# Perceiver of four layers on one core: the first tile's rows, queries, later constants and weights are put in another order where three cross-attentions open

## Chip, cores and metric

The kernel runs on one core of one Trainium2 chip, in fp32. The metric is the device time of one execution in microseconds (us). Engines are named as in the profile: PE (TensorE, matmuls), DVE (VectorE), ACT (ScalarE), POOL (GpSimd), SP (SyncE, which here only issues DMAs). L12 is line 12 of the kernel before; where a line of the changed kernel is meant, the text says so.

## What is computed

The input is x with 16 batches of 64 rows of 256 (1024 tokens) and a context of 16 batches of 1024 rows of 192. Four layers follow each other, each of three parts that add to x:

```python
x = x + L1_xattn(layernorm(x), ctx, ...)   # 16 heads over 1024 keys of the batch
x = x + L1_attn(layernorm(x), ...)
x = x + L1_ffn(layernorm(x), ...)          # 8 experts, top 1
x = x + L2_xattn(layernorm(x), ctx, ...)   # 8 heads of 64
x = x + L2_attn(layernorm(x), ...)         # complex linear recurrence over 64 rows
x = x + L2_ffn(layernorm(x), ...)          # 8 experts, top 2, capacity 160
x = x + L3_xattn(layernorm(x), ctx, ...)   # 8 heads of 64
x = x + L3_attn(layernorm(x), ...)         # convolution, state space with 16 states
x = x + L3_ffn(layernorm(x), ...)          # three dense layers of +1/-1 weights
```

Layer 0 is built alike; its ffn takes the top 2 of 8 experts and adds a shared expert. So each of the three later cross-attentions comes straight after a feed-forward part with experts.

## The kernel before

The tokens lie in SBUF as `xs`, 8 tiles of 128 (two batches each). A feed-forward part with experts writes its results, sorted by expert, to HBM (`ys`). The next stage brings them back: `carry(i)` (L1388) gathers tile i's rows by an indirect DMA that POOL issues (L1386), one per expert choice, two after layer 0 and layer 2 and one after layer 1, and DVE adds each, weighted by its gate, to `xs` (L1395). Then `norm_tile` makes the layernorm's numbers (DVE L154, L156, L158; POOL L160, a power), DVE writes the normalized tile `o`, POOL adds the attention's bias to `xs`, PE transposes `o` (L179), and an evict on DVE or ACT in turn (L62, L64) brings it to SBUF as `hT`.

`L1_xattn` (the opening at L1014) makes, for batch 0, four pieces: `keys(0)`, `values(0)`, `keys(1)`, `values(1)` (matmuls L926, L928 and L940, L947; evicts to `kT` and `v`), with the three turns of `queries(0)` (carry, norm and `o`; transposes and `hT`; matmuls, `qs` and the two DMAs of `qs` L907 that turn it to other partitions) after the second, third and fourth piece. In this opening the order of PE and DVE instructions is the written one, in the loop that follows that of PE only; all other orders are chosen by a scheduler that runs over the program with its own costs, so it may hoist the later tiles' gathers and adds. The loop has 64 steps (16 batches of 4 groups of heads): scores (`sc`, L69), `nmx` on DVE (L223), `p` on ACT (L225), transposes (L235) and their copies `pT` (DVE L239, ACT L237), averages. Batch b+1's four pieces are spread over the steps of batch b, one a step, but step 0 also takes one before its scores. `queries(1)` and `queries(2)` are also given their turns in these steps. The gathered rows rest in four buffers (`back`).

`heads64` (L431) is the cross-attention of layers 2 and 3. For a tile, `normalized(i)` does carry, norm and transposes (the o of all tiles is one buffer), `queries(i)` the matmuls to `qT` (DVE L470), `with_keys(i, n)` turns them by the key weights to `qp` (twice, evicts L62 and L64), then scores with the context itself (L505). In layer 2 (`L2_xattn_attn`, L1728) the stage of the recurrence is made first (`recurrence`, L1739: powers on POOL L1749 and L1752, a chain of small DVE steps L1751 to L1769 and L1781 to L1792 that wraps angles, sine and cosine on ACT) and its steps are then woven in by calls from within heads64. In layer 3 (`state_space`) a block of matmuls, `first()` (32 of them, evicts ACT L1986), goes first; `weights()` issues six DMAs on SP: `L3a_in` 1 MB, `L3a_bc` 64 KB, `L3a_out` 512 KB (L1990) and `k0` 512 KB, `k1` 1 MB, `k2` 256 KB (L1910). Nothing makes these wait but the rooms they write to.

Of the kernel before, what the change touches and what calls it, by code (L numbers as in the profile page):

```python
# [11 lines left out]
F32 = mybir.dt.float32  # L12
# [30 lines left out]
class Net:  # L43
# [387 lines left out]
    def heads64(  # L431
# [5 lines left out]
        nc = self.nc  # L437
        wq, wkT, wv0, wv1, wo, bo, (sels, rb, vT), self.spent = self.pack()
        large = large or self.misc
        qpT, hT = {}, {}  # L440

        nc.gpsimd.iota(
            sels.rearrange("p h (r d) -> p h r d", r=2), pattern=[[1, 4], [32, 2], [0, 64]], base=0,
# [6 lines left out]
        def normalized(i):  # L450

            if i < 2:
                self.carry(i, self.lp.tile([128, 4, D], F32, tag="p", bufs=2, name="p"))
            else:
                self.carry(i, tag="o", bufs=1)
            mv, rs = self.norm_tile(self.xs[:, i, :], 1e-5)
            o = self.lp.tile([128, D], F32, tag="o", bufs=1, name="o")
            nc.vector.tensor_scalar(o, self.xs[:, i, :], mv[:, 0:1], rs, ALU.subtract, ALU.mult)
            nc.gpsimd.tensor_tensor(self.xs[:, i, :], self.xs[:, i, :], bo, ALU.add)
            hT[i] = self.lp.tile([128, 2, 128], F32, tag="hT", bufs=2, name="hT")  # L460
            self.evict(hT[i], self.transposed(o))
# [391 lines left out]
    def L1_xattn(self):  # L853
# [26 lines left out]
            self.mm(ps, [(bv[:, c, :], wo[:, c, :]) for c in range(2)] + [(self.ones[:1, :], bo)])  # L880
            nc.scalar.copy(bias, ps)

        qs = {}

        def queries(i):

            self.carry(i)
            mv, rs = self.norm_tile(self.xs[:, i, :], 1e-5)
            o = self.lp.tile([128, D], F32, tag="o", bufs=2, name="o")
            nc.vector.tensor_scalar(o, self.xs[:, i, :], mv[:, 0:1], rs, ALU.subtract, ALU.mult)  # L890
            nc.gpsimd.tensor_tensor(self.xs[:, i, :], self.xs[:, i, :], bias, ALU.add)
            yield
            hT = self.lp.tile([128, 2, 128], F32, tag="hT", bufs=2, name="hT")
            self.evict(hT, self.transposed(o))
            yield
            ps = self.misc([128, 2, 128])
            for m in range(2):
                self.mm(ps[:, m, :], [(wq[:, c, m * 128 : (m + 1) * 128], hT[:, c, :]) for c in range(2)])
            qs[i] = [self.lp.tile([128, 2, 2, 2, S], F32, tag=f"qs{n}", bufs=3, name=f"qs{n}") for n in range(2)]
            for m in range(2):  # L900
                for h in range(2):
                    nc.vector.tensor_scalar(
                        qs[i][0][:, m, :, h, :], ps[:, m, :].rearrange("p (b s) -> p b s", s=S),
                        self.col("L1x_bq", m), self.pair4[:, h : h + 1], ALU.add, ALU.mult,
                    )
            for r in range(2):
                nc.sync.dma_start(qs[i][1][64 * r : 64 * r + 64], qs[i][0][64 - 64 * r : 128 - 64 * r])  # L907
            yield
# [102 lines left out]

        self.room_t = self.misc

        with self.tc.manual_schedule(engines={mybir.EngineType.PE, mybir.EngineType.DVE}):  # L1014
            biases()
            for piece, turn in zip(keys_values(0), (None, *[queries(0)] * 3)):
                piece()
                if turn is not None:
                    next(turn)
        with self.tc.manual_schedule(engines={mybir.EngineType.PE}):  # L1020
            held, work = None, {}
# [3 lines left out]
            for k in range(len(steps) + 4):  # L1025
# [5 lines left out]
                if k < len(steps):  # L1031
                    b, g = steps[k]
                    if not g:
                        sums = self.lp.tile([128, 8], F32, tag="sums", bufs=3, name="sums")
                        more = keys_values(b + 1) if b + 1 < B else None
                    if not k:
                        more.pop(0)()
                    now = (b, g, scores(b, g, sums), sums)
                for piece in work.pop((k, "early"), ()):
                    piece()  # L1040
# [344 lines left out]
    def gather_rows(self, out, src, at):  # L1385
        return self.nc.gpsimd.indirect_dma_start(out, None, src, bass.IndirectOffsetOnAxis(ap=at, axis=0))  # L1386

    def carry(self, i, room=None, tag="back", bufs=4):  # L1388

        if self.routed is None:  # L1390
            return
        for n, (at, g) in enumerate(zip(self.routed.at, self.routed.gates)):
            y = self.lp.tile([128, D], F32, tag=tag, bufs=bufs, name="back") if room is None else room[:, n, :]
            self.gather_rows(y, self.ys, at[:, i : i + 1])
            self.nc.vector.scalar_tensor_tensor(  # L1395
                self.xs[:, i, :], y, g[:, i : i + 1], self.xs[:, i, :], ALU.mult, ALU.add
            )
# [331 lines left out]
    def L2_xattn_attn(self):  # L1729


        with self.tc.manual_schedule(engines={mybir.EngineType.PE}):
            lru = self.recurrence()
            self.heads64(breathe=lru.go, finished=lru.more)
            self.start_pack(self.at)
            while lru.go():
                pass

    def recurrence(self):  # L1739
        nc = self.nc  # L1740
        s = SimpleNamespace(ready=0, next=0, work=None)
        w = []
# [2 lines left out]
        at = VEC_AT["L2a_logs"]  # L1745
        logs = self.vecs[:, at : at + 3]
        e1 = self.lp.tile([128, 3], F32, name="e1")
        nc.vector.memset(e1, float(np.e))
        nc.gpsimd.tensor_tensor(ex[:, :3], e1, logs, ALU.pow)  # L1749
        neg = self.lp.tile([128, 1], F32, name="neg")  # L1750
# [199 lines left out]
    def state_space(self):  # L1950
# [35 lines left out]
                nc.scalar.copy(w[1][:, :, cols], ps)  # L1986

        def weights():
            for n, to in zip(("in", "bc", "out"), (w[0], w[2], w[3])):
                nc.sync.dma_start(to, self.a[f"L3a_{n}"])  # L1990
            yield
            self.ffn = self.fetch_L3_ffn((self.spent[0], w[4], self.spent[1]))
            yield

        def prepare(k):
# [508 lines left out]
```

## Time and profile before

| what | us |
|---|---|
| three runs | 2837.02, 2842.88, 2844.15 |
| median | 2842.88 |
| the profiled execution | 2838.53 |
| its span, first to last instruction | 2836.7 |
| PE's busy time in it | 2603.1 |
| opening of L1's cross-attention, first keys to the second nmx | 438.4 to 476.3 |
| opening of L2's, last write of expert rows to the first scores | 1221.0 to 1243.9 |
| opening of L3's, the same | 1931.6 to 1959.7 |

The granted clock of TensorE over the span was 0.963 of full. A row of a timeline gives start, duration, engine, line, operation, output and inputs, the number of instructions in it, and in brackets the idle time of the engine before it with what ended it. A row of the DMA view gives the count, the size of each and the median time from issue to landing. An entry of the chain gives the start, the duration and what the end of the kernel hung on in that time.

### The profile page before, as it was taken

The numbers are of one execution on the slowest core, as the hardware profiler recorded it, in microseconds if no ns is written. First come the engines' busy times: TensorE is split into PE (matmuls) and PEld (weight loads), VectorE is DVE, ScalarE is ACT, GpSimd is POOL, SyncE is SP. The second block draws the span as 40 slices with busy tenths as digits, with TensorE's granted clock in tenths as the row PEclk, the third lists the DMA queues.
The fourth block names the chain that finished last, engine by engine and source line by source line (L and its number), as shares of the span: only waits on it lengthen the run. The fifth ranks groups of instructions, "written<-read, shape, count | busy, mean of one in ns | idle before, by whom it ended". The sixth has DMA issues, their size and how long they took to land.

```text
span 2836.7 us, 44734 instructions
## 1 busy us (share of the span) xinstructions
PE 2603.1 (92%) x18116; PEld 1889.9 (67%) x18116; DVE 1399.4 (49%) x2825; ACT 1003.4 (35%) x2114; POOL 311.8 (11%) x429
## 2 busy tenths in 40 slices
PE   7888998999999898979999999698999998998999
PEld 3556895666666686856666666695666665666777
DVE  3556225666666643233434342423344756658692
ACT  1323223555555441222222222122234545455330
POOL 1111333000000112310001000201001000000000
PEclk9988999999999997989999999799999999999999
DMA  8512872100100114801111111463112213121110
GB/s 244 174 49 77 339 271 65 31 27 28 38 27 23 42 38 176 305 25 47 59 58 55 45 49 59 181 239 108 51 49 91 86 49 97 56 76 30 61 45 8
DMA packets 79228, 253.71 MB, mean 89 GB/s; under 512 B 15151, under 2 KB 26954, under 8 KB 69290
## 3 DMA queue, kind: packets, MB, share of 16 engines
q1 hardware_dynamic: 59562, 165.01, 18.0%
q0 software_dynamic: 13312, 80.28, 7.9%
q10 hardware_dynamic: 6144, 5.51, 0.6%
q8 instruction: 145, 2.38, 0.3%
q14 instruction: 65, 0.53, 0.1%
HBM read 233.80 MB, written 14.82 MB: 88 GB/s over the span
## 4 chain that ended last, share of the span: by engine, by line
PE 38%; DVE 9%; ACT 3%; issue 2%; DMA 2%; POOL 1%; SPq 1%; DVEq 0%; ACTq 0%; POOLq 0%
PE sc L505 9%; PE ps_h L69 5%; PE misc L541 4%; PE halves L69 3%; PE misc L69 3%; PE ps_t L519 3%; PE halves L541 3%; PE misc L536 2%; PE gu L69 2%; DVE x L2104 2%; PE halves L2128 2%; PE halves L536 1%; DVE nmx L223 1%; DVE x L2100 1%; DMA rep<-dus 1%
## 5 line engine op out<-in xcount | busy, mean ns | idle before, releaser
L223 DVE TENSOR_REDUCE nmx<-sc 128x1 f32<-128x1024 f32 x264 | 311.7, 1218 | 228.4 <-PE sc L505 144.8
L225 ACT ACTIVATE p<-sc,nmx 128x1024 f32<-128x1024 f32 x264 | 294.2, 1115 | 313.5 <-DVE nmx L223 313.3
L505 PE MATMUL sc<-ctxT,qp 128*128 128x512 f32 (+1 forms) x1024 | 357.5, 603 | 0.0
L505 PEld LDWEIGHTS sc<-ctxT,qp 128*128 128x128 f32 (+1 forms) x1024 | 139.4, 190 | 155.4 <-issue 152.3
L519 PE MATMUL ps_t<-ident,p 128*128 128x128 f32 x1024 | 140.2, 279 | 40.2 <-ACT pT L522 17.3
L2094 ACT ACTIVATE da<-rep,al 128x252 f32<-128x252 f32 x256 | 115.9, 500 | 134.4 <-DVE x L2104 124.2
L519 PEld LDWEIGHTS ps_t<-ident,p 128*128 128x128 f32 x1024 | 115.3, 142 | 65.2 <-ACT pT L522 21.0
L2104 DVE TENSOR_TENSOR_SCAN x<-da,x 128x512 f32<-128x512 f32 x128 | 152.7, 1218 | 2.7 <-ACT da L2094 1.9
L235 PE MATMUL misc<-ident,p 128*128 128x128 f32 x1024 | 137.1, 279 | 7.2 <-ACT p L225 6.8
L522 ACT COPY pT<-ps_t 128x512 f32<-128x512 f32 x166 | 94.0, 587 | 122.0 <-PE ps_t L519 116.1
L235 PEld LDWEIGHTS misc<-ident,p 128*128 128x128 f32 x1024 | 110.1, 141 | 32.7 <-ACT p L225 15.4
L160 POOL TENSOR_TENSOR ln_rs<-ln_ve,nhalf 128x1 f32<-128x1 f32 x80 | 44.9, 567 | 692.8 <-DVE ln_ve L158 611.0
L541 PE MATMUL halves<-pT,ctx 128*128 128x256 f32 x512 | 119.3, 386 | 0.0
L541 PE MATMUL misc<-pT,ctx 128*128 128x256 f32 x512 | 119.1, 386 | 0.0
L237 ACT COPY pT<-misc 128x512 f32<-128x512 f32 x128 | 75.0, 586 | 108.6 <-PE misc L235 108.1
L69 PE MATMUL ps_h<-r,w 128*128 128x256 f32 x512 | 113.4, 381 | 0.0
L2100 DVE TENSOR_TENSOR x<-rep,bc_rep 128x512 f32<-128x512 f32 x128 | 84.7, 687 | 57.9 <-PE halves L2128 55.2
L239 DVE COPY pT<-misc 128x512 f32<-128x512 f32 x128 | 88.3, 690 | 39.7 <-PE misc L235 28.6
L69 PEld LDWEIGHTS ps_h<-r,w 128*128 128x128 f32 x512 | 96.6, 190 | 15.9 <-issue 2.5
L541 PEld LDWEIGHTS halves<-pT,ctx 128*128 128x128 f32 x512 | 94.8, 190 | 17.3 <-issue 5.6
L541 PEld LDWEIGHTS misc<-pT,ctx 128*128 128x128 f32 x512 | 94.6, 190 | 17.1 <-issue 5.5
L69 PE MATMUL po<-wb,hid 128*128 128x256 f32 x440 | 100.3, 379 | 0.0
(500 smaller groups left out, 4504.3 us busy)
## 6 DMA issues: line engine op xcount, KB each, us to landing
ctx<-in_ctx SPq DMA_DIRECT2D x48, 768.0 KB, 4.4
ctxT<-in_ctxT SPq DMA_DIRECT2D x48, 512.0 KB, 3.3
w<-in_L2f_W SPq DMA_DIRECT2D x24, 1024.0 KB, 8.3
rep<-dus SPq DMA_DIRECT2D x256, 64.0 KB, 1.9
ctxT<-in_ctxT SPq DMA_DIRECT2D x16, 768.0 KB, 15.5
ctxT<-in_ctxT SPq DMA_DIRECT2D x96, 128.0 KB, 3.5
ys<-yb ACTq DMA_DIRECT2D x40, 128.0 KB, 5.7
bc_rep<-bcs SPq DMA_DIRECT2D x32, 128.0 KB, 3.0
```

Of the source, the lines that this page charges most:

```text
L69: self.nc.tensor.matmul(out, lhsT, rhs, start=n == 0, stop=n == len(pairs) - 1)
L223: self.nc.vector.tensor_reduce(nmx, sc, AX.X, ALU.max, negate=True)
L225: self.nc.scalar.activation(p, sc, AF.Exp, bias=nmx, accum_out=sums)
L235: self.nc.tensor.transpose(ps[:, u, :], p[:, at : at + 128], self.ident)
L239: self.nc.vector.tensor_copy(pT[:, 0:4, :], ps)
L505: nc.tensor.matmul(sc[u][:, bass.ts(kh, 512)], qp[n][par][rows, h : h + 2, :].rearrange("p h q -> p (h q)"), ctx[0][rows, at], start=n == ...
L519: nc.tensor.transpose(ps[:, t, :], p[:, at : at + 128], self.ident)
L522: nc.scalar.copy(to, ps)
L541: nc.tensor.matmul(o, ck[:, t, :128], pT[:, t].rearrange("p u q -> p (u q)"), start=t == 0, stop=t == NK - 1)
L2094: nc.scalar.activation(da[:, g, :, 1:], now[j][:, 0, :].rearrange("p (b s) -> p b s", s=S)[:, :, 1:], AF.Exp, scale=al[:, col : col + 1],)
L2100: nc.vector.tensor_tensor(h, now[j][:, 1:2, :].to_broadcast([128, 2, CHUNK]), bc[:, 0, states, :], ALU.mult)
L2104: nc.vector.tensor_tensor_scan(flat, da.rearrange("p g b s -> p (g b s)"), flat, 0.0, ALU.mult, ALU.add)
```

## The change

Five edits. `carry` gets an argument `behind`: if it is given, DVE first copies one column of that tile into the room of the gathered rows, so that the gather cannot be issued before that tile exists. heads64 gives tile 1's carry the `o` of tile 0; L1_xattn gives tiles 1 and 2 the `o` of the tile before. In L1_xattn's opening POOL too keeps the written order, and the first turn of `queries(0)` stands ahead of `keys(0)`, the second after `values(0)`, the third after `keys(1)`. In its loop, step 0 no longer takes a piece of batch 1 before its scores, so that steps 0 to 3 take one each. In layer 2 the recurrence is made at the first call from within heads64, and its constant `e1` is first written with a piece of tile 1's `xs`. In layer 3 DVE copies a column of tile 0's `xs` into each of the six rooms before the weights' DMAs. In all DVE has 14 more instructions (4 + 1 + 2 for `behind`, 1 for `e1`, 6 for the rooms), each of one column of 128 or of 128x3; matmuls, transfers and other instructions are the same.

```diff
--- before.py
+++ after.py
@@ -437,7 +437,7 @@
         nc = self.nc
         wq, wkT, wv0, wv1, wo, bo, (sels, rb, vT), self.spent = self.pack()
         large = large or self.misc
-        qpT, hT = {}, {}
+        qpT, hT, os = {}, {}, []
 
         nc.gpsimd.iota(
             sels.rearrange("p h (r d) -> p h r d", r=2), pattern=[[1, 4], [32, 2], [0, 64]], base=0,
@@ -450,11 +450,12 @@
         def normalized(i):
 
             if i < 2:
-                self.carry(i, self.lp.tile([128, 4, D], F32, tag="p", bufs=2, name="p"))
+                self.carry(i, self.lp.tile([128, 4, D], F32, tag="p", bufs=2, name="p"), behind=os[-1] if os else None)
             else:
                 self.carry(i, tag="o", bufs=1)
             mv, rs = self.norm_tile(self.xs[:, i, :], 1e-5)
             o = self.lp.tile([128, D], F32, tag="o", bufs=1, name="o")
+            os.append(o)
             nc.vector.tensor_scalar(o, self.xs[:, i, :], mv[:, 0:1], rs, ALU.subtract, ALU.mult)
             nc.gpsimd.tensor_tensor(self.xs[:, i, :], self.xs[:, i, :], bo, ALU.add)
             hT[i] = self.lp.tile([128, 2, 128], F32, tag="hT", bufs=2, name="hT")
@@ -880,13 +881,13 @@
             self.mm(ps, [(bv[:, c, :], wo[:, c, :]) for c in range(2)] + [(self.ones[:1, :], bo)])
             nc.scalar.copy(bias, ps)
 
-        qs = {}
+        qs, os = {}, {}
 
         def queries(i):
 
-            self.carry(i)
+            self.carry(i, behind=os[i - 1] if 0 < i < 3 else None)
             mv, rs = self.norm_tile(self.xs[:, i, :], 1e-5)
-            o = self.lp.tile([128, D], F32, tag="o", bufs=2, name="o")
+            os[i] = o = self.lp.tile([128, D], F32, tag="o", bufs=2, name="o")
             nc.vector.tensor_scalar(o, self.xs[:, i, :], mv[:, 0:1], rs, ALU.subtract, ALU.mult)
             nc.gpsimd.tensor_tensor(self.xs[:, i, :], self.xs[:, i, :], bias, ALU.add)
             yield
@@ -1011,11 +1012,15 @@
 
         self.room_t = self.misc
 
-        with self.tc.manual_schedule(engines={mybir.EngineType.PE, mybir.EngineType.DVE}):
+        with self.tc.manual_schedule(
+            engines={mybir.EngineType.PE, mybir.EngineType.DVE, mybir.EngineType.Pool}
+        ):
             biases()
-            for piece, turn in zip(keys_values(0), (None, *[queries(0)] * 3)):
+            turn = queries(0)
+            next(turn)
+            for n, piece in enumerate(keys_values(0)):
                 piece()
-                if turn is not None:
+                if 0 < n < 3:
                     next(turn)
         with self.tc.manual_schedule(engines={mybir.EngineType.PE}):
             held, work = None, {}
@@ -1033,8 +1038,6 @@
                     if not g:
                         sums = self.lp.tile([128, 8], F32, tag="sums", bufs=3, name="sums")
                         more = keys_values(b + 1) if b + 1 < B else None
-                    if not k:
-                        more.pop(0)()
                     now = (b, g, scores(b, g, sums), sums)
                 for piece in work.pop((k, "early"), ()):
                     piece()
@@ -1385,12 +1388,14 @@
     def gather_rows(self, out, src, at):
         return self.nc.gpsimd.indirect_dma_start(out, None, src, bass.IndirectOffsetOnAxis(ap=at, axis=0))
 
-    def carry(self, i, room=None, tag="back", bufs=4):
+    def carry(self, i, room=None, tag="back", bufs=4, behind=None):
 
         if self.routed is None:
             return
         for n, (at, g) in enumerate(zip(self.routed.at, self.routed.gates)):
             y = self.lp.tile([128, D], F32, tag=tag, bufs=bufs, name="back") if room is None else room[:, n, :]
+            if behind is not None:
+                self.nc.vector.tensor_copy(y[:, :1], behind[:, :1])
             self.gather_rows(y, self.ys, at[:, i : i + 1])
             self.nc.vector.scalar_tensor_tensor(
                 self.xs[:, i, :], y, g[:, i : i + 1], self.xs[:, i, :], ALU.mult, ALU.add
@@ -1730,10 +1735,16 @@
 
 
         with self.tc.manual_schedule(engines={mybir.EngineType.PE}):
-            lru = self.recurrence()
-            self.heads64(breathe=lru.go, finished=lru.more)
+            made = []
+
+            def lru():
+                if not made:
+                    made.append(self.recurrence())
+                return made[0]
+
+            self.heads64(breathe=lambda place: lru().go(place), finished=lambda i: lru().more(i))
             self.start_pack(self.at)
-            while lru.go():
+            while lru().go():
                 pass
 
     def recurrence(self):
@@ -1745,6 +1756,7 @@
         at = VEC_AT["L2a_logs"]
         logs = self.vecs[:, at : at + 3]
         e1 = self.lp.tile([128, 3], F32, name="e1")
+        nc.vector.tensor_copy(e1, self.xs[:, 1, :3])
         nc.vector.memset(e1, float(np.e))
         nc.gpsimd.tensor_tensor(ex[:, :3], e1, logs, ALU.pow)
         neg = self.lp.tile([128, 1], F32, name="neg")
@@ -1986,10 +1998,13 @@
                 nc.scalar.copy(w[1][:, :, cols], ps)
 
         def weights():
-            for n, to in zip(("in", "bc", "out"), (w[0], w[2], w[3])):
+            rooms = w[0], w[2], w[3], self.spent[0], w[4], self.spent[1]
+            for to in rooms:
+                nc.vector.tensor_copy(to[:, 0, :1], self.xs[:, 0, :1])
+            for n, to in zip(("in", "bc", "out"), rooms):
                 nc.sync.dma_start(to, self.a[f"L3a_{n}"])
             yield
-            self.ffn = self.fetch_L3_ffn((self.spent[0], w[4], self.spent[1]))
+            self.ffn = self.fetch_L3_ffn(rooms[3:])
             yield
 
         def prepare(k):
```

## The prediction

> **What bounds the kernel now.** I read the page first, then its chain of work that ended last, then the timelines of the three places where the change acts.
>
> ```profile
> PE 2603.1 (92%) x18116; PEld 1889.9 (67%) x18116; DVE 1399.4 (49%) x2825; ACT 1003.4 (35%) x2114; POOL 311.8 (11%) x429
> ...
> PE 38%; DVE 9%; ACT 3%; issue 2%; DMA 2%; POOL 1%; SPq 1%; DVEq 0%; ACTq 0%; POOLq 0%
> ```
>
> TensorE is busy 92% of the span, so the change can only win idle time of PE, and a stretch is lost only if PE (or what feeds it) stands longer. The change leaves the number of matmuls as it is; the order of instructions in the two programs differs only in the first 40 to 70 us of the three later cross-attentions. I call these opening 1 (436 to 476 us), opening 2 (1221 to 1244) and opening 3 (1930 to 1960). Their idle PE time is what can be won.
>
> Opening 1, PE's timeline (start, duration, engine, line; in brackets the idle time before and its releaser):
>
> ```profile
> 448.96 1.13 PE L928 MATMUL misc<-ctxT,w 64*128 64x512 f32 x4
> 454.77 0.66 PE L179 MATMUL misc<-ident,o 128*128 128x128 f32 x2 [4.68 <-DVE o L890]
> 455.22 3.62 PE L940 MATMUL misc<-w,ctxT 128*128 128x256 f32 x8
> ...
> 463.73 1.13 PE L69 MATMUL sc<-kT,qs 32*128 32x512 f32 x4
> 467.07 1.13 PE L69 MATMUL sc<-kT,qs 32*128 32x512 f32 x4 [2.21 <-DMA qs<-qs]
> ```
>
> PE has done the keys and stands 4.68 us for tile 0's o, then 2.21 us for the second half of the queries. Why o is late shows in DVE's timeline: the gather that tile 0 needs was issued at 438.82, but its add waits behind work for tiles 1 and 2.
>
> ```profile
> 448.95 0.47 DVE L1395 SCALAR_TENSOR_TENSOR xs<-back,route_g,xs 128x256 f32<-128x256 f32 x1
> 450.05 0.88 DVE L1395 SCALAR_TENSOR_TENSOR xs<-back,route_g,xs 128x256 f32<-128x256 f32 x2 [0.63 <-DMA back<-ys,route_at]
> ...
> 454.16 0.47 DVE L890 TENSOR_SCALAR o<-xs,ln_mv,ln_rs 128x256 f32<-128x256 f32 x1 [1.47 <-POOL ln_rs L160]
> ...
> 469.11 2.35 DVE L223 TENSOR_REDUCE nmx<-sc 128x1 f32<-128x1024 f32 x2
> ...
> 476.28 2.36 DVE L223 TENSOR_REDUCE nmx<-sc 128x1 f32<-128x1024 f32 x2 [0.86 <-PE sc L69]
> ```
>
> Each step of the loop begins with an nmx on DVE; the second one (476.28) is my finishing line for opening 1.
>
> Openings 2 and 3, from the chain of work in order of time: the same write of expert rows (128 KB in opening 2, the last 32 KB in opening 3) lands in 1.76 us in one, and in 8.25 us in the other, where 2.6 MB of weights are on their way.
>
> ```profile
> 1221.04 1.76 DMA ys<-yb
> ```
> ```profile
> 1932.07 8.25 DMA ys<-yb
> ```
>
> PE in opening 3: a block of 32 matmuls that needs no row of tile 0 covers the wait until 1945.16, and 4.24 us are left open.
>
> ```profile
> 1931.26 13.90 PE L69 MATMUL large<-w_dt,w_xT 128*128 128x512 f32 x32
> 1949.39 0.44 PE L179 MATMUL halves<-ident,o 128*128 128x128 f32 x2 [4.24 <-DVE o L458]
> 1950.39 3.65 PE L69 MATMUL large<-hT,w 128*128 128x128 f32 x16 [0.56 <-issue]
> ```
>
> PE in opening 2: 12.47 us idle for tile 0's o.
>
> ```profile
> 1232.95 0.66 PE L179 MATMUL misc<-ident,o 128*128 128x128 f32 x2 [12.47 <-DVE ln_mv L156]
> 1234.12 3.46 PE L69 MATMUL misc<-hT,w 128*128 128x128 f32 x16 [0.52 <-DVE hT L62]
> 1238.37 1.16 PE L69 MATMUL misc<-qT,w 64*128 64x128 f32 x16 [0.78 <-DVE qT L470]
> 1240.44 2.40 PE L69 MATMUL misc<-qT,w 64*128 64x128 f32 x16 [0.91 <-DVE qp L62]
> ```
>
> **Opening 1, step by step.** Tile 0's gathers keep their issue times (437.56, 438.82) and land 2.8 us later, 441.65. Add 0.45, stats 0.41, aggregate 0.16, ve 0.13, pow 0.58, o 0.45 with small gaps: o ends near 444.15 instead of 454.6. Its transposes then stand on PE behind values(0) (446.6), so the 4.68 us gap goes. Next late is tile 1: its two gathers now wait for o(0) and for two copies of one column (0.14 each by the 128x1 row of L158), are issued at 445.2 and 446.5 and land at 449.3; the copy of v on DVE stands behind their adds, so the query matmuls start at 450.6. kT's second piece then waits for o(1) (pow on POOL in between) and ends at 453.65, values(1) runs 453.7 to 457.8, the qs DMAs go at 455.15. The first scores are ready 8 us earlier. But DVE's order puts nine adds, those of tiles 1 to 4 and one of tile 5, ahead of the first nmx. Tile 2's gathers wait for o(1) (452.5); each costs POOL 0.95 plus 0.30 to the next, so tile 5's first is issued near 460 to 462 and its row lands 2.8 us later uncontended, or 4.0 to 5.3 where the 768 KB of ctxT (issued 458.87 to 461.57) run beside it. First nmx: 465.9 to 467.3, 2 to 3 us earlier than 469.11. The second stands behind adds of tiles 5 and 6 that sit between the copies of pT: 475 to 477.5 against 476.28. Last, one piece of batch 1's keys and values moves from step 0 to step 3. Steps with a piece are 7.14 to 7.36 us apart, the one without (492.60 to 498.78) 6.18, so it costs 1.0 there; in step 0 it lay in part under the 2.21 us wait. Sum: between −1.5 and +3, and I take **+0.3**. The end below, if nothing were queued ahead of the nmx: scores complete about 461.3, 7.8 earlier, less 1.0 for the piece, −6.8.
>
> **Opening 2.** The constants' chain (pow at 1224.70, then eleven small DVE steps from 1225.63) leaves its place ahead of tile 0's add, which began at 1229.99 though its row landed about 1226.5. Add, norm and o end at 1228.95 instead of 1232.8, transposes 1229.0, hT by 1230.1, queries from 1230.15 instead of 1234.12: 4.0 earlier. Their result qT then stands on DVE behind tile 1's add, norm and o. That gather, now behind o(0), goes at 1229.95 instead of 1226.87 and lands 1232.75; o(1) ends 1235.15, qT 1235.9, and with_keys comes 2.4 earlier (1235.95 against 1238.37). Now the constants' chain comes: it waits for tile 1's xs, costs two pows (0.89 and 0.59) and the small steps again, and stands ahead of qp's copy until 1239.8. Second with_keys: 1240.25 against 1240.44. The activation table for sine is loaded later (1.28 on ACT), under matmuls. Result −0.2 to −0.75, ends −2.4 (nothing queued) and +1 (the chain takes 1.2 longer, as one POOL gap of 1.27 did): **−0.5**.
>
> **Opening 3.** Without weights on the way, ys lands 1.76 after 1932.07, at 1933.85. Tile 0's gathers go 0.75 later (1934.6, 1935.9), the second lands 1938.6, o ends 1941.05: 8 us earlier, all under the 13.9 us block, so only what passes 1945.16 counts. Six one-column copies on DVE (6 × 0.14 = 0.8) and the bias add on POOL (0.72) come next, and the 3.4 MB of weights are issued from 1942.0; their first reader is at 2113, so their lateness costs nothing. Tile 1's gathers now wait for o(0): 1942.05 and 1943.3, that is, into the start of the weights. tile 0's hT (transposes end at 1945.9) stands on DVE behind tile 1's adds and statistics. With L the landing of tile 1's second row, queries start at L + 1.92. Uncontended (2.7, the row below): L = 1946.1, queries 1948.0, −2.3. The nearest row for a gather issued into a weight stream is the hb gather of the stage before:
>
> ```profile
> hb<-hs,tokens POOLq DMA_INDIRECT x7, 6.5
> ```
> ```profile
> p<-ys,route_at POOLq DMA_INDIRECT x4, 2.7
> ```
>
> 5.3 to 7.0 gives queries at 1950.5 to 1952.2, 0.1 to 1.8 late. If it takes the 8.25 of ys, +3.1. The break-even is a landing of 5.2 us. I take 5.9, as the stream is only starting: **+0.8**. If hT were not queued, the end is 1945.16 plus 0.4, −4.2.
>
> A row that speaks to both: 8.25 us for a write beside weights, 1.76 alone. The Trainium skill, "DMA: Bandwidth & Descriptors", section Rules for kernel authors, says the opposite of this edit: issue a DMA early and wait late. By that rule holding back 3.4 MB would cost; by the row the early weights cost ys 6.5 us, and the trace decides for the row. The same page, section Issuing engines are not separate DMA queues, has all queues interleave on the same 16 engines; by it the collision is only moved onto tile 1's rows.
>
> **Sum:** +0.3 − 0.5 + 0.8 = **+0.6 us**. The profiled execution took 2838.53 us (span 2836.7 plus 1.8), so 2839.1; the median of the three runs is 2842.88, 4.35 higher, lowest 2837.02. I forecast between the two bases, **2840**. About 0.3%, 8.5 us, is what a measurement of this kernel can tell from no change.
>
> **Rivals.**
> 1. *The queues don't bind* (faster): DVE's rows come in time, and the gaps go. −5 in opening 1 (of the cap 6.8), −2 in opening 2, −3 in opening 3: −10, 2829; all three ends −6.8 − 2.4 − 4.2 = −13.4, 2825. For it: gaps of 4.68, 2.21, 12.47 and 4.24 us on PE whose releaser is tile 0. Against it: the adds of later tiles keep their place in DVE's order. Chance 0.33.
> 2. *Rows one after another* (slower): DVE works in order, so a row fetched later holds up tile 0's own next step. Place: tile 1's second add in opening 3, tile 5's first in opening 1. If ys lands late all the same (8.25, because of something other than the weights), o(0) ends 1949.3, tile 1's gathers go near 1949.6 and 1950.8, land 1953.5, queries 1955.4: +5.0; with +3 in opening 1 and +1 in opening 2, +9, 2848 from the profiled execution, 2852 from the median. It decides from a landing above 5.2 us in opening 3. For it: the hb row. Against it: ys alone took 1.76. Chance 0.17.
> 3. *It doesn't do what it says*: the collision only moves and the first scores begin when they did; the three sums stay within ±1.5 each. That is near my forecast, and its price is 2838 to 2844. With the forecast 0.50.
>
> **How the numbers follow.** Faster 0.33, same 0.50, slower 0.17. The likeliest case alone spans 2836 to 2846. The range reaches from 2829, the middle of rival 1, to 2849, within rival 2: it leaves out some 0.1 on each side.
>
> **What would show it.** In the profile after: in opening 1 no idle before L179 and o near 444; the first nmx 466 to 467, the second near 476; step 3 longer by 1. In opening 2 tile 0's add near 1226.5 and queries 4 earlier, second with_keys nearly unmoved. In opening 3 ys landing under 3 us and DVE waiting for tile 1's rows with hT behind. Wrong if the second nmx of opening 1 moves by over 3 us, or if tile 1's rows in opening 3 land in under 4.

## Result and profile after

The changed kernel takes 2846.24 us (median of 20 runs, 2838.07 to 2850.35), the kernel before 2841.20 (20 runs, 2832.97 to 2845.26): ratio 1.0019, 95% interval 1.0012 to 1.0025, so 5 us or 0.2% slower, with an interval that leaves out 1. My sum was +0.6 us and my forecast 2840. The profiled execution took 2843.67 us, its span 2841.8.

The page of the kernel after, the lines that answer to those shown of before:

```profile
PE 2602.9 (92%) x18116; PEld 1888.9 (66%) x18116; DVE 1403.4 (49%) x2839; ACT 1001.8 (35%) x2114; POOL 312.1 (11%) x429
...
PE 40%; DVE 9%; ACT 3%; issue 2%; DMA 2%; POOL 1%; SPq 1%; ACTq 0%; DVEq 0%; POOLq 0%
```

PE does the same matmuls in the same busy time; DVE has the 14 instructions more. What changed is where PE stands idle, so each opening has to be measured from a mark to a mark. I use: **opening 1** from the first matmul of the biases (`misc<-w,bv`, L69) to the fifth nmx (so that the piece moved from step 0 to step 3 is inside), **opening 2** from the last `po<-wb,hid` matmuls to the third pair of nmx, **opening 3** from the small transposes `pr` to the third nmx, which opens the second pair. Where an expectation below speaks of another mark, it says so.

| us | before | after | difference |
|---|---|---|---|
| opening 1: first, second, fifth nmx | 32.57, 39.74, 62.24 | 32.19, 41.35, 66.09 | −0.38, +1.61, +3.85 |
| opening 2: third pair of nmx | 62.41 | 64.01 | +1.60 |
| opening 3: first, third nmx | 34.16, 44.86 | 36.55, 46.92 | +2.39, +2.06 |

The start of opening 1 lies 4.78 us earlier in the trace of after, that of opening 2 1.09 later, of opening 3 2.36 later; before opening 1 both run the same program, so this offset is the spread of executions. Below, "shifted" means a time of before plus this offset.

**Opening 1**, PE's timeline of after:

```profile
452.06 1.13 PE L69 MATMUL sc<-kT,qs 32*128 32x512 f32 x4
454.28 1.13 PE L69 MATMUL sc<-kT,qs 32*128 32x512 f32 x4 [1.10 <-DMA qs<-qs]
...
457.25 1.13 PE L929 MATMUL misc<-ctxT,w 64*128 64x512 f32 x4
466.46 1.12 PE L235 MATMUL misc<-ident,p 128*128 128x128 f32 x4 [8.07 <-ACT p L225]
468.19 2.82 PE L235 MATMUL misc<-ident,p 128*128 128x128 f32 x12 [0.62 <-DVE ln_ve L158]
470.94 2.09 PE L69 MATMUL sc<-kT,qs 32*128 32x512 f32 x8
```

The two gaps of before (4.68 for o, 2.21 for qs) have gone, the scores are complete 8 us earlier, and in their place stands one gap of 8.07 us ahead of the first transposes, whose p waits for nmx. DVE's timeline shows what nmx stands behind:

```profile
438.93 0.41 DVE L891 TENSOR_SCALAR o<-xs,ln_mv,ln_rs 128x256 f32<-128x256 f32 x1 [0.69 <-POOL ln_rs L160]
...
457.00 0.88 DVE L1400 SCALAR_TENSOR_TENSOR xs<-back,route_g,xs 128x256 f32<-128x256 f32 x2 [4.53 <-DMA back<-ys,route_at]
...
463.95 2.34 DVE L223 TENSOR_REDUCE nmx<-sc 128x1 f32<-128x1024 f32 x2
...
473.11 2.35 DVE L223 TENSOR_REDUCE nmx<-sc 128x1 f32<-128x1024 f32 x2 [0.78 <-PE sc L69]
```

DVE idles 4.53 us for a later tile's rows with finished scores behind it. The stretch table (stretch, length, busy time and instructions of PE, PEld, DVE, ACT and POOL, then granted clock, DMA share, GB/s) shows the second effect of the long gap:

```profile
466.00:470.00 4.00, 2.93 (x13) 2.53 (x14) 3.97 (x13) 2.69 (x6) 2.21 (x3) 0.50 0.25 74
470.00:474.00 4.00, 4.00 (x16) 1.99 (x15) 2.99 (x7) 0.58 (x1) 1.26 (x2) 0.50 0.00 0
```

After PE has stood 8 us the granted clock is 0.50 for about 8 us: 16 transposes and 8 score matmuls take 1.12 + 2.82 + 2.09 = 6.03 us, in before 0.66 + 1.53 + 1.14 = 3.33:

```profile
472.75 0.66 PE L235 MATMUL misc<-ident,p 128*128 128x128 f32 x4
473.60 1.53 PE L235 MATMUL misc<-ident,p 128*128 128x128 f32 x12 [0.19 <-DVE v L62]
475.06 1.14 PE L69 MATMUL sc<-kT,qs 32*128 32x512 f32 x8
```

**Opening 2**, PE and POOL of after:

```profile
1230.26 0.66 PE L179 MATMUL misc<-ident,o 128*128 128x128 f32 x2 [8.69 <-DVE o L459]
1231.44 3.78 PE L69 MATMUL misc<-hT,w 128*128 128x128 f32 x16 [0.52 <-DVE hT L62]
1239.57 2.08 PE L69 MATMUL misc<-qT,w 64*128 64x128 f32 x16 [4.35 <-DVE qT L471]
1243.97 2.40 PE L69 MATMUL misc<-qT,w 64*128 64x128 f32 x16 [2.33 <-DVE qp L62]
```
```profile
1233.45 1.01 POOL L1389 DMA_INDIRECT p<-ys,route_at  x1 [2.53 <-issue]
```

The same gather in before:

```profile
1226.87 1.01 POOL L1386 DMA_INDIRECT p<-ys,route_at  x1 [1.27 <-issue]
```

Queries start 3.8 us earlier (shifted); then PE waits 4.35 us for qT, which stands on DVE behind tile 1's add, and tile 1's gather was issued late: POOL stood 2.53 us ahead of it with nothing in the trace to wait for.

**Opening 3**, DVE and PE of after:

```profile
1950.27 0.48 DVE L1400 SCALAR_TENSOR_TENSOR xs<-p,route_g,xs 128x256 f32<-128x256 f32 x1 [5.49 <-DMA p<-ys,route_at]
1951.96 0.48 DVE L1400 SCALAR_TENSOR_TENSOR xs<-p,route_g,xs 128x256 f32<-128x256 f32 x1 [1.21 <-DMA p<-ys,route_at]
```
```profile
1953.74 3.75 PE L69 MATMUL large<-hT,w 128*128 128x128 f32 x16 [6.01 <-issue]
1958.33 2.08 PE L69 MATMUL large<-qT,w 64*128 64x128 f32 x16 [0.83 <-issue]
...
1964.11 6.37 PE L506 MATMUL sc<-ctxT,qp 128*128 128x512 f32 x16
```

Tile 1's rows, issued at 1944.45 and 1945.75 into the start of the weights, reach their adds 5.8 and 6.2 us later; hT stands behind them on DVE, and PE idles 6.01 us (4.24 in before). Again the clock is 0.50 in the 10 us that follow; in before it was 0.66 and 0.73. The stretches of after, then those of before:

```profile
1954.00:1959.00 5.00, 4.17 (x22) 3.90 (x24) 1.10 (x2) 0.00 (x0) 0.81 (x3) 0.50 0.24 95
1959.00:1964.00 5.00, 4.11 (x32) 3.60 (x31) 0.95 (x3) 1.24 (x4) 0.00 (x0) 0.50 0.02 3
```
```profile
1950.00:1955.00 5.00, 3.77 (x18) 3.55 (x20) 1.40 (x3) 0.00 (x0) 1.50 (x5) 0.66 0.00 0
1955.00:1960.00 5.00, 4.12 (x35) 3.66 (x36) 1.43 (x4) 1.44 (x5) 0.00 (x0) 0.73 0.01 3
```

### The profile page after: what moved, and what is told of

It reads as the page before. It is cut to its first block, busy times and chain, and to the rows that moved or that the text cites. A ratio compares the mean times of both kernels' runs of the same rounds, so it can differ in the third digit from the quotient of the medians.

```text
span 2841.8 us, 44773 instructions
## 1 busy us (share of the span) xinstructions
PE 2602.9 (92%) x18116; PEld 1888.9 (66%) x18116; DVE 1403.4 (49%) x2839; ACT 1001.8 (35%) x2114; POOL 312.1 (11%) x429
## 4 chain that ended last, share of the span: by engine, by line
PE 40%; DVE 9%; ACT 3%; issue 2%; DMA 2%; POOL 1%; SPq 1%; ACTq 0%; DVEq 0%; POOLq 0%
PE sc L506 9%; PE ps_h L69 5%; PE misc L542 4%; PE halves L69 3%; PE misc L69 3%; PE ps_t L520 3%; PE halves L542 3%; PE gu L69 2%; PE misc L537 2%; DVE x L2119 2%; PE halves L2143 2%; PE halves L537 2%; DVE nmx L223 1%; PE po L69 1%; PE large L69 1%
## 5 line engine op out<-in xcount | busy, mean ns | idle before, releaser
L69 PE MATMUL ps_h<-r,w 128*128 128x256 f32 x512 | 113.4, 381 | 0.0
L69 PEld LDWEIGHTS ps_h<-r,w 128*128 128x128 f32 x512 | 96.6, 190 | 15.9 <-issue 2.5
L69 PE MATMUL po<-wb,hid 128*128 128x256 f32 x440 | 100.5, 379 | 0.1
```

The costliest lines, as they stand in the source:

```text
L69: self.nc.tensor.matmul(out, lhsT, rhs, start=n == 0, stop=n == len(pairs) - 1)
```

## Experiments

My theory after the result: **the waits do free tile 0 and hide the gain, because the rows that now come later stand on DVE ahead of tile 0's next step**; and PE's longer unbroken gap costs clock on top. The rivals: the moved piece is what costs in opening 1; the transfers that now collide cost, not the queue; the order around them (recurrence, weights) costs.

| kernel | ratio to before, 95% interval | opening 1 | opening 2 | opening 3 |
|---|---|---|---|---|
| after | 1.0019, 1.0012 to 1.0025 | 66.09 | 64.01 | 46.92 |
| no_behind | 0.9990, 0.9978 to 1.0002 | 64.93 | 62.54 | 39.79 |
| lazy_weights | 0.9988, 0.9977 to 0.9999 | 65.25 | 64.75 | 39.90 |
| two_pieces | 1.0025, 1.0015 to 1.0036 | 67.48 | 64.10 | 46.90 |
| bulk_later | 1.0009, 1.0000 to 1.0018 | 63.64 | 65.49 | 46.15 |
| adds_later | 1.0010, 0.9996 to 1.0024 | 62.62 | 64.09 | 46.75 |
| gate_weights | 0.9986, 0.9972 to 1.0001 | 63.45 | 62.80 | 39.63 |
| warm3 | one run, 2844.16 us | 64.25 | 62.78 | 49.71 |
| open1_alone | one run, 2847.86 us | 65.87 | 62.83 | 44.82 |
| weights_only | 0.9988, 0.9978 to 0.9998 | 65.49 | 62.88 | 39.68 |
| piece_kept | one run, 2847.80 us | 68.57 | 65.29 | 47.34 |
| open2_alone | one run, 2844.37 us | 62.63 | 65.16 | 44.54 |
| open3_rows | one run, 2848.29 us | 62.17 | 63.12 | 49.70 |

**no_behind**: the changed kernel without the copies that hold back the later tiles' gathers.

```diff
-            if behind is not None:
-                self.nc.vector.tensor_copy(y[:, :1], behind[:, :1])
```

> The changed kernel without the copies that make later tiles' gathers wait (nothing else undone). Opening 1 is measured from the biases' first matmul to the fifth nmx (62.2 us before, 66.1 changed), opening 2 from the last write of expert rows to the second pair of nmx (40.5 and 42.2), opening 3 from the small transposes ahead of the block of 32 matmuls to the second pair of nmx (44.9 and 46.9). Theory (rows fetched one tile after another, in DVE's fixed order, hold up the first tile, and the longer unbroken idle of PE lowers its clock): opening 1 60 to 63, opening 2 37 to 38.5, opening 3 38 to 41; time 0.995 to 0.998 of before. Rival (bulk loads beside the gathers make the rows late): opening 1 stays at 65 or more, since the context is still loaded early. Rival (the piece moved to step 3): opening 1 stays above 64.

Opening 3 falls from 46.92 to 39.79, 7 us under after and 5 under before, and the kernel goes from 1.0019 to 0.9990. `behind` is what costs in opening 3. Opening 2 took 62.54, as in before, but lazy_weights, which has the same instructions there, took 64.75: one trace does not tell what `behind` costs in opening 2. Opening 1 missed the 60 to 63 that I expected, and the time its 0.995 to 0.998. In opening 1 the first nmx does not come earlier without it (33.21): there something else holds the nmx (adds_later shows what).

**lazy_weights**: the kernel before with two of the five edits, weights that wait and the recurrence made at the first call.

```diff
+            self.heads64(breathe=lambda place: lru().go(place), finished=lambda i: lru().more(i))
...
+            for to in rooms:
+                nc.vector.tensor_copy(to[:, 0, :1], self.xs[:, 0, :1])
```

> The kernel before with two parts of the change alone: the recurrence's constants wait for tile 1's xs, and the weights of layer 3 wait for tile 0's xs. No gather waits for another tile, opening 1 as before. Theory: opening 1 62.2; opening 2 37 to 38.5, since tile 0's add and the key matmuls come 3 us earlier; opening 3 38 to 41, as the write of rows takes 1.8 instead of 8.25 us, all four gathers land before the weights start, and PE's idle shrinks to about 1 us; time 0.995 to 0.998 of before. Rival (holding back weights or constants is itself the loss): openings 2 and 3 at 42 and 46 or more, time above before.

Opening 3 at 39.90, opening 2 no better (64.75), ratio 0.9988, short of the 0.995 to 0.998 that I expected. Opening 1 has the program of before in this kernel and yet took 65.25: one trace of an opening is worth about ±2 us. The last section comes back to this.

**two_pieces**: step 0 takes one piece of batch 1 more, after its scores, into the 8.07 us gap.

```diff
                     if more:
                         more.pop(0)()
+                    if not k:
+                        more.pop(0)()
```

> The changed kernel, but step 0 of the loop takes two pieces of batch 1 after its scores, so step 3 takes none as before. Rival (the moved piece): opening 1 64.1 or less, as step 3 gets back the 2.0 us by which it is longer and step 0 had 8 us of idle PE for the piece; the clock after it drops less. If only the queue and the clock count: 66, with the first nmx unmoved in both. I expect 63.5 to 64.5, so that the piece accounts for half of the loss of opening 1; time 0.9995 of the changed kernel, 1.0012 of before.

It got worse: 67.48, ratio 1.0025. The gap cannot take the piece. PE of two_pieces:

```profile
470.93 2.93 PE L941 MATMUL misc<-w,ctxT 128*128 128x256 f32 x6 [7.39 <-DVE ln_ve L158]
```

The matmuls need PSUM (the memory that they write to) that DVE empties, and its copy (kT, 470.14 to 470.88) stands behind the same adds; PE waits in the middle of the piece instead of after it.

**bulk_later**: the changed kernel with the context's load of opening 1 held until batch 1's first keys are ready, and layer 3's weights held for tile 1's xs.

```diff
+            if b == 2:
+                late = self.ctxT[self.ctx_n % 2].rearrange("p c k -> p (c k)")
+                nc.vector.tensor_copy(late[:, :1], kv[1][0][:, 0, :1])
...
-                nc.vector.tensor_copy(to[:, 0, :1], self.xs[:, 0, :1])
+                nc.vector.tensor_copy(to[:, 0, :1], self.xs[:, 1, :1])
```

> The changed kernel with the bulk loads moved out of the rows' way: the six weights of layer 3 wait for tile 1's xs instead of tile 0's, and the 512 KB part of batch 2's context waits for batch 1's first keys. Gathers still wait for the tile before. Rival (bulk loads): opening 1 62 to 63.5 with the first nmx 27.5 to 29 after the biases (32.2 changed); opening 3 42 to 43. Theory (serial rows): opening 1 64 to 66, first nmx 30 to 32, since nine rows still stand ahead of it; opening 3 42 to 44, shorter than before only by what the landing saves.

First nmx 30.70 (after 32.19), fifth 63.64. In this pair the transfer beside the gathers is worth 1.5 us, so most of the wait is something else (adds_later, next, shows what). In opening 3 the first nmx comes 5 us earlier (31.58 against 36.55), but the third comes at 46.15: the weights now stream beside the gather of tile 2, whose row reaches its add 5.64 us after the issue (2.85 in after). That misses the 42 to 44 that I expected.

**adds_later**: in opening 1, the weight of each row of tiles 2 and later is gate + 0·(sums of step 0), so that DVE can do these adds only after the first step.

```diff
+                self.nc.vector.scalar_tensor_tensor(
+                    share, later[:, :1], 0.0, g[:, i : i + 1], ALU.mult, ALU.add
+                )
```

> The changed kernel, with the adds of tiles 2 to 7 in opening 1 made to wait for step 0's sums (their gate is added to zero times a sum), so that none of them stands ahead of the first nmx on DVE. Gathers go as in the changed kernel. Theory (DVE's order): the first nmx comes 24 to 25.5 us after the biases (32.2 in the changed kernel, 32.6 before), PE's 8 us of idle shrink to 2 or less, and opening 1 takes 61 to 64 (66.1). Rival (the landing of rows beside the context's load): the first nmx hardly moves, as the scores themselves are late. Time 0.9985 to 0.9995 of the changed kernel.

The first nmx comes at 23.84 instead of 32.19. So the queue on DVE is what holds it, and not PE, qs or the transfer. But from the first nmx to the second it is 11.45 us, from there to the third 10.77, and the fifth nmx is at 62.62. PE of adds_later, between the second and the third nmx:

```profile
468.10 2.79 PE L235 MATMUL misc<-ident,p 128*128 128x128 f32 x12 [4.51 <-DVE v L62]
```

The same adds now stand ahead of a copy of v. Of 8.35 us at the first nmx, 3.5 are left at the fifth in this pair of traces; the kernel went from 1.0019 to 1.0010, with 1 inside its interval.

**gate_weights**: lazy_weights, and in opening 2 tile 1's add (not its gather) waits for tile 0's o.

```diff
+                    share, behind[:, :1], 0.0, g[:, i : i + 1], ALU.mult, ALU.add
```

> The kernel before with the weights of layer 3 waiting for tile 0's xs, the recurrence's constants waiting for tile 1's xs, and in opening 2 tile 1's add (not its gather) waiting for tile 0's o. Theory: tile 0's o as early as in the changed kernel (queries 14 after the last matmuls), but tile 1's row lands meanwhile, so the first key matmuls come 3 us earlier than before and the third pair of nmx at 58.5 to 60.5 (62.4 before, 64.0 changed); opening 3 39.8. Time 0.9965 to 0.9985 of before. Rival (the wait is POOL's: about 2 us ahead of the second gather of this stage in every trace, whatever is put there): the gain of opening 2 is under 1.

Opening 2 stays at 62.80. With the add out of the way qT stands behind the recurrence's constants on DVE instead, and PE waits 2.89 us for it. So the gain of opening 2 is under 1, as my rival had it, and POOL again stood 2.05 us ahead of the second gather; but the wait that PE shows is that for qT. Ratio 0.9986, not to be told from lazy_weights.

**warm3**: 12 matmuls whose result nothing reads, put on PE into the gap of opening 3.

```diff
+            for _ in range(12):
+                nc.tensor.matmul(ps.rearrange("p m f -> p (m f)"), x[:, 0, :128], dt[:, 0, :], start=True, stop=True)
```

> The changed kernel with 12 matmuls whose result nobody reads after tile 0's transposes in opening 3, in the 6.0 us in which PE stands idle. If the lowered clock after that idle is part of the price, the queries' 16 matmuls take about 2.0 instead of 3.75 us and the two groups of key matmuls 1.2 instead of 2.08 and 2.40, and the third nmx comes at 43 to 45 instead of 46.9. If the clock has no part, 46.9 or later.

PE of warm3 (L2005 is the filler, two instructions for each matmul):

```profile
1944.50 10.46 PE L2005 MATMUL large<-w_dt,w_xT 128*128 128x512 f32 x24
1954.80 1.95 PE L69 MATMUL large<-hT,w 128*128 128x128 f32 x16
...
1973.52 7.07 PE L506 MATMUL sc<-ctxT,qp 128*128 128x512 f32 x16
```

The filler was larger than the gap (10.46 us against 6), so queries start 24.74 after pr, 4.1 later than in after; yet the first nmx comes at 35.95 against 36.55. From the start of the queries to the first nmx it is 11.21 us at full clock (granted 1.00), 15.93 in after, 14.53 in before. The lowered clock thus costs 4.7 us of this stretch in after, 1.4 more than it cost before. The third nmx (49.71) does not profit and misses the 43 to 45 that I expected: the second group of scores runs slowly in its turn, 7.07 us where after has 5.52. Whether a filler of the right size would win is not settled.

**open1_alone**: the kernel before with opening 1 changed alone; 2 and 3 are the old ones.

```diff
-                if turn is not None:
+                if 0 < n < 3:
...
-                    if not k:
-                        more.pop(0)()
```

> The kernel before with the edits of opening 1 alone. A second sample of both: opening 1 as changed (66.1 seen once, 67.5 and 63.6 in relatives), openings 2 and 3 as before (62.4 to the third pair of nmx, 44.9). I expect opening 1 between 64 and 67.5, step 3 at 8.2 instead of 6.2, opening 3 within 0.3 of before, opening 2 within 2.5 of it, since the clock's window falls anew in each run.

Opening 1 at 65.87, as in after, its step 3 again 8.19 us; openings 2 and 3 (62.83, 44.82) as in before. The parts add up place by place, and opening 1's part is a loss.

**weights_only**: the kernel before with only the six copies that hold the weights.

```diff
+            for to in rooms:
+                nc.vector.tensor_copy(to[:, 0, :1], self.xs[:, 0, :1])
```

> The kernel before with one edit alone: the six one-column copies that make layer 3's weights wait for tile 0's xs. Theory: opening 3 39.6 to 39.9 as in the other two kernels in which no gather waits (44.9 before), openings 1 and 2 as before (62.2 to 65.3, 62.4 to 62.8). Time 0.9975 to 0.999 of before, 5 us. Rival (the rows' write lands early, but the weights then take the gain back further down): time 0.9995 or more.

Opening 3 at 39.68, ratio 0.9988 (0.9978 to 0.9998), 2837.36 us against 2840.85 beside it: this one edit alone has a lower ratio than the five together, and its interval lies below 1. PE of weights_only:

```profile
1951.24 2.02 PE L69 MATMUL large<-hT,w 128*128 128x128 f32 x16 [0.56 <-ACT w L1986]
...
1957.84 5.52 PE L505 MATMUL sc<-ctxT,qp 128*128 128x512 f32 x16
```

All four gathers have landed before the weights start, PE stands only 0.56 us ahead of the queries, and these run in 2.02 us instead of 3.65. Part of this comes back at once: the first nmx is 7.7 us earlier than in before, the third 5.2, as the second group of scores takes 7.21 us instead of 5.52. As opening 3 gains 5.1 and the whole 3.4 (interval 0.6 to 6.3), some of it may be given back later; the runs don't tell.

**piece_kept**: the changed kernel with the piece of batch 1 back ahead of step 0's scores.

```diff
+                    if not k:
+                        more.pop(0)()
```

> The changed kernel with the piece of batch 1's keys kept ahead of the first scores in step 0, as before. Step 3 (fourth to fifth nmx) 6.2 instead of 8.2. If the piece fits into PE's 8 us of idle, opening 1 takes 63.5 to 64; if step 0's values then wait for PSUM, which DVE frees only after the nine adds (7.4 us of idle with two pieces after the scores), 65.5 to 67.5. I expect the latter.

The step from the fourth to the fifth nmx is 6.18 again (8.19 in after), so the moved piece costs 2.0 there. But the first nmx goes from 32.19 to 37.30, because the piece too needs copies that stand behind DVE's adds, and the end is 68.57, over the 65.5 to 67.5 that I expected: once the queries go first, the piece costs more in its old place.

**open2_alone**: the kernel before with opening 2 changed alone: the recurrence made at the first call, and tile 1's gather behind tile 0's o.

```diff
-            self.heads64(breathe=lru.go, finished=lru.more)
+            self.heads64(breathe=lambda place: lru().go(place), finished=lambda i: lru().more(i))
...
+        nc.vector.tensor_copy(e1, self.xs[:, 1, :3])
```

> The kernel before with the edits of opening 2 alone: constants after tile 1's xs, tile 1's gather after tile 0's o. Opening 2: third pair of nmx at 63.5 to 65.5 (64.0, 64.1, 64.1, 65.5 and 62.8 in kernels with the same edits, 62.4 and 62.8 without). POOL stands 2.5 us ahead of the second gather, after tile 0's o. If the stall were chance, the gather would follow within 0.3 us of the bias add, and 62 or less. Opening 1 62 to 65.5, opening 3 44.9, as before.

Opening 2 at 65.16 (before 62.41), the others as before, and POOL stood 2.53 us ahead of the second gather, as expected. Alone too it does not gain.

**open3_rows**: the kernel before with `behind` in opening 3 alone, the weights early as before.

```diff
+            if behind is not None:
+                self.nc.vector.tensor_copy(y[:, :1], behind[:, :1])
```

> The kernel before with tile 1's gathers of layer 3 waiting for tile 0's o, and nothing else: the weights go early, so the write of rows takes about 8.25 us. This is the slower rival of the prediction, which priced it at 5.0 us: queries 24.6 after the small transposes (19.6 before), third nmx 49 to 52 with the clock lower for longer (44.9 before). If rows one after another cost nothing by themselves, 44.9 to 46.

The chain of work, and PE, of open3_rows:

```profile
1935.78 7.79 DMA ys<-yb
```
```profile
1957.78 3.75 PE L69 MATMUL large<-hT,w 128*128 128x128 f32 x16 [6.38 <-issue]
```

Queries 23.3 us after pr (before 19.6), third nmx 49.70. So in opening 3 `behind` alone costs 4.8, the weights' wait alone wins 5.1, and both together cost 2.1 to 2.2, because the weights, which start after tile 0's xs, then stream while tile 1's held rows are gathered.

## Why the prediction was right or wrong

Means over all traces with the same program in an opening take out most of its scatter:

| | as before | as after | difference |
|---|---|---|---|
| opening 1 | 63.5 (six traces, 62.17 to 65.49) | 65.4 (three, 64.25 to 66.09) | +1.9 |
| opening 2 | 62.8 (four, 62.41 to 63.12) | 64.4 (seven, 62.78 to 65.49) | +1.6 |
| opening 3 | 44.7 (three, 44.54 to 44.86) | 47.0 (four, 46.75 to 47.34) | +2.2 |

Their sum, +5.7, agrees with the measured +5.0 (medians) to +5.4 (ratio). My terms were +0.3, −0.5 and +0.8. That for opening 3 failed by 1.4, for opening 1 by 1.6, for opening 2 by 2.1. The steps that failed are these: the moved piece of opening 1, priced at 1.0 and measured at 2.0; the issue of opening 2's second gather, which made all that hangs on it 2.4 us late where I had −0.2; and in opening 3 the slow matmuls behind PE's gap, for which I had no term.

- **Right: tile 0 comes earlier and gains nothing.** o of opening 1 ends at 439.34 (predicted 444.15, shifted 439.37), the scores are complete 8.0 earlier, opening 2's queries 3.8 (predicted 4.0), o of opening 3 ends at 1943.48 (predicted 1941.05, shifted 1943.41). That DVE's order hides this in opening 1 is shown by adds_later, in opening 3 by no_behind. Rival 1 is out.
- **Right: opening 3's landing.** Predicted 5.9, measured 5.8 and 6.2 up to the adds; queries +0.8 predicted (the terms written there give 0.7), +1.0 measured. The landing passed the break-even of 5.2, so rival 2's mechanism decided, though at a smaller price than its +5.0: ys did land early once the weights waited (last write issued at 1934.4, first gather released 1936.90; 1932.07 and 1941.09 in before). open3_rows has the case that rival 2 priced, ys still late (7.79): queries 3.7 late where it said 5.0.
- **Wrong: opening 3 ended with the start of the queries.** I had no term for PE's clock. From queries to the first nmx, the same matmuls cost 1.4 us more in after, behind a gap of 6.01 instead of 4.24 us; four kernels without such a gap, and warm3, take 11.2 to 11.3 us for them. In the mean of the traces in the table it is 1.1: three of four with the gap of 6 us took 15.9 to 16.1 and one, piece_kept, 14.1; those with the program of before took 14.2 to 14.5.
- **Wrong in size: the moved piece.** Step 3 got longer by 2.0, not 1.0, and this accounts for opening 1's loss: in the means of the same traces the first nmx comes 1.6 earlier, the second 0.1 earlier, the fifth 1.9 later. My 1.0 compared steps of 7.14 to 7.36 that hold a piece but no queries with one of 6.18 that holds the matmuls of queries(2) (1.16 us) instead. The step ahead of that one holds both, and its 8.83 us stood in the trace of before.
- **Right in part: the first nmx of opening 1**, predicted 2 to 3 us earlier, came 0.38 earlier in this pair, 1.6 in the mean (33.5 to 32.0). The chain of single landings was right up to o(1) (448.1; predicted 452.5, shifted 447.7), but the context's load went out at 451.61, 2.5 us sooner than in my account, right among the gathers. Those issued at 451.62, 452.87 and 454.12 took 5.4, 6.0 and 5.1 us (the others 2.7 to 3.1); the rooms came free late, and by count tile 5's first gather left at 459.00 instead of 455 to 457 (shifted). bulk_later gives 1.5 of this back.
- **Right in number, for two reasons: the second nmx of opening 1**, predicted between 1.3 earlier and 1.2 later, 1.6 later in this pair and 0.1 earlier in the mean. The later tiles' adds do stand there, as I said: DVE works on them and their statistics until 472.33. Then it waits 0.78 us for scores that run at half clock, so of the clock's 2.7 us I estimate that about 1 reaches this nmx. For that I had no term.
- **Wrong: opening 2's second gather.** I had it at 1229.95 (shifted 1231.04); it left at 1233.45. POOL's 1.27 us of "issue" in front of the same gather stood in the trace of before, and I used it only as the far bound (+1). It is 2.0 to 2.5 us wherever the constants no longer lie between the two gathers (2.53 after, 2.04 no_behind, 2.05 lazy_weights). Row, qT, the constants' chain and qp then all came 2.4 later: second with_keys +2.44 instead of −0.2.
- **The rule weighed there.** Holding back 3.4 MB won 3.4 us (weights_only, interval 0.6 to 6.3). The rule of the Trainium skill, "DMA: Bandwidth & Descriptors", section Rules for kernel authors, to issue early and wait late, did not hold for a load that streams beside a short write and its readback.

The numbers for the chances stood on sums of terms near zero, each the difference of a gain and a new wait. All three errors had one sign and added up to 5.1 us; the time lies in the stated range because that was wide.

Open: what POOL does in those 2 us; the means, from three to seven traces each; what `behind` and the constants cost singly in opening 2; whether weights_only's last 1.7 us are lost or only scatter.

## What to carry to other kernels

When a tile is put first, look at what the engine that works in order has queued ahead of its next step: a held-back row that lands later takes its place in that queue, and the wait moves instead of going. Of a set of edits that each take or add a wait, price each alone: here one (the weights' wait) won 5 us in its place, and another (`behind`) lost them and more in the same place. To price work that moves, take from the trace a step that is like the new one in all else. A gap on TensorE costs its length and the slow matmuls after it; both belong in the sum.

## What the runs showed of the hardware

- **Granted clock.** After the gap of 8.07 us the clock was 0.50 for some 8 us, after that of 6.01 us for over 10. Behind short gaps it varied from run to run. The second half of step 0's scores in opening 1 and the eight matmuls of values that follow, in weights_only and then in open3_rows, which have the same instructions there:

```profile
464.43 2.08 PE L69 MATMUL sc<-kT,qs 32*128 32x512 f32 x4 [1.85 <-DMA qs<-qs]
466.44 3.78 PE L940 MATMUL misc<-w,ctxT 128*128 128x256 f32 x8
```
```profile
465.80 1.13 PE L69 MATMUL sc<-kT,qs 32*128 32x512 f32 x4 [1.92 <-DMA qs<-qs]
466.86 1.99 PE L941 MATMUL misc<-w,ctxT 128*128 128x256 f32 x8
```

In before the eight took 2.85. This is most of the ±2 us by which one trace of opening 1 differs from another: these two are 65.49 and 62.17, and the 3.3 us between them are there at the second nmx already (42.98 and 39.67). The Trainium skill, "TensorE: Matmul & The Clock Gate", section What's actually happening, has half clock after an idle window of about 3.4 us and a window that runs freely, which agrees with the two long gaps and with the spread; the half clock behind 1.85 us of idle is not covered by an idle window of that length, and the measurement stands. The same section puts the ramp at under 1% of a span and advises against fitting a count of slow matmuls. Here it is 4.7 us in opening 3, under 0.2% of the span, and as much as the whole effect of the change, though 3.3 of it were there before the change too.
- **Two gaps or one.** Against the same matmuls at full clock, those behind the two gaps of before in opening 1 (4.68 and 2.21 us) took 3.5 us more (eight L940 twice, 3.62 and 2.85 against 1.99, and some smaller rows), those behind the one of after (8.07 us) 3.3 more (the 2.7 above and 2.59 against 1.99). This is an estimate from single rows of two traces; it does not show one long gap to be dearer than two short ones.
- **A short write beside a bulk load.** The 32 KB of ys took 8.25 us (before) and 7.79 (open3_rows) while weights streamed. Where they waited (after), the first gather followed the issue of the write by 2.5 us, against 9.0 in before; less the 0.8 between landing and gather there, that is a landing of some 1.7, an estimate.
- **POOL ahead of a second indirect DMA** stood 2.0 to 2.5 us in layer 2 (1.27 behind a power), and 0.30 in the other openings, for a cause that the trace does not name.
